# Mask products behind waits on relus and sums, query copies on ScalarE, ranking scratch in another block

## The chip, the cores and the metric

The kernel runs on one core of a Trainium2 chip. A core has five engines with a queue each, worked off in order: TensorE (PE in the profile, with PEld for its weight loads), VectorE (DVE), ScalarE (ACT), GpSimd (POOL) and SyncE (SP, which here only issues DMAs). The engines run at the same time and wait for each other through semaphores. The metric is the device time of one execution in microseconds (us).

## The reference

Two layers on x of shape (2, 256, 64, 64), that is two images of 256 channels and N = 4096 positions. Cut to what matters:

```python
# layer 0: sparsemax attention over the positions
e = prelu(batchnorm(conv3x3(x)))            # 64 channels
sim = einsum('bdn,bdm->bnm', e, e)
sim = sim - max(sim, axis=2)
tau = ...                                   # from the sorted row
p = maximum(sim - tau, 0)
x = einsum('bcn,bnm->bcm', x, p) + x
# layer 1: non-local block
g = g_w x + g_b
a, bsc = query and key scalar of each position   # one number each
f = relu(a[:, :, None] + bsc[:, None, :] + wf_b)
y = (f / N) g
z = batchnorm(wz_w y + wz_b) + x
```

## The kernel before

**What it does for the reference.** A position whose row of `sim` has one large entry only, its own, has a row of `p` that is 1 on the diagonal; layer 0 then gives 2x in that column. The kernel surveys all rows, lists the others (up to 384 an image, three blocks of 128, `KB`), and computes only those exactly. A mask per image holds 2 for the positions that are not listed and 1 for those that are. The output of layer 0 is x times the mask plus what the listed rows add. In layer 1 the relu of a sum of two scalars is worked out without the N x N matrix: keys are ranked, sums of g over the ranked keys are made into a table, and each query fetches one row of the table. In image 1 only 16 of 32 blocks of keys (`NR`) are ranked; the other 16 go through a dense product (`pair_f` on ACT, `pair_py` on PE).

**The order of the work.** No order is written out by hand. The kernel makes a few thousand tasks (`plan.task`), each with a cost on one or two engines, a rank, the tasks it comes after and the buffers it takes; `Plan.run` goes through them in the order of a modelled time and emits the instructions. Of the tasks that could start at about the same time the one with the lowest rank is taken. The ranks of the stages are the twenty numbers `DB, CV1, LS, RW0, ...`. So any new rank, cost or dependency can move instructions on every queue. On the chip only the data dependencies and the order within each queue hold; a task's place in the plan's `after` list makes no wait by itself.

**The stages**, image 0 first, image 1 overlapped with it:

- `conv` and `thresholds`, then `survey` (PE products `sv`, DVE running maxima L524 and row maxima L533, ACT row sums L528).
- `listed`: the list of rows. It writes the mask to DRAM and loads it back over all partitions (`keep_out`, `keep_in` L671, L678), and gathers the listed rows of e and x by indirect DMAs on POOL (L710, L714).
- `rows`: PE products `rw` of the listed rows, ACT copies them into `z_0`, `z_1`, `z_2` (L789), DVE takes eight maxima (L792), `threshold(k)` turns them into a bias `nb` by nine small DVE instructions (L796 to L806, among them the 8-wide `tensor_scalar` of L798), and `relu` (L812 on ACT or L814 on DVE) applies it.
- `doubled`: POOL multiplies x by the mask, eight products of 128 x 1024 an image (L764). In the plan they come after the mask and all relus. The instruction itself reads x and the mask only.
- `attend`: PE products `av` of z (L838), and for each of 8 column blocks and 2 channel halves one DVE sum `into` (L845), which adds the product to x and so waits for the mask product of its columns.
- `project`: g, the key and query scalars (`ga`) by PE (L869 for image 0, L895 for image 1) and DVE (L875, L906).
- `Ranked`: `turn` (L1020, L1021) copies the query column of `ga` and its negative; `keys` (L994 to L1008) makes the keys; they go through PE (`pt_k`, L920), ACT (`row_k`, L924), DRAM (`rd_k`) and come back over all partitions as `kb` (L940). `above` counts, for each block of 128 keys, the keys above it, either on ACT (L1032) or on DVE (L1037, a `tensor_scalar` that also sums up); `ties` (L1051, a DVE instruction with two SBUF inputs) counts equal keys; `place` makes ranks; `scatter` (L1072) writes the rows to DRAM in order of rank. Then `load`, `products`, `sums`, `raised`, `stored` make the table, `segments`, `places`, `counts` find each query's row, `fetch` (L1158) gathers it on POOL, and `taken` and `finish` make the output (L1171 to L963).

**Buffers.** The large tiles share seven blocks, S0 to S6, and a new tile in a block waits for the last use of the one before. Before the change S6 holds the mask of image 0 and then `ga_0`; S3 holds the fourth conv input of both images, later the table of image 1; S5 holds `e_1` (read until the last `rw` of image 1), then the scratch `junk_0` of the ranking of image 0 and then `rest`, the dense part of image 1. The products `rw` of the listed rows use S0, S1, S2 and S4 for z.

Of the kernel before, what the change touches and what calls it, by code (L numbers as in the profile page):

```python
# [8 lines left out]
F32 = mybir.dt.float32  # L9
BF16 = mybir.dt.bfloat16  # L10
# [4 lines left out]
ALU = mybir.AluOpType  # L15
# [4 lines left out]
P = 128  # L20
HW = 64
N = HW * HW
CB = 512
NCB = N // CB
NT = N // P
CT = 2
# [164 lines left out]
def sparse_path(ctx: ExitStack, tc, a, out, rows_i):  # L191
# [89 lines left out]
    DB, CV1, LS, RW0, SV1, RW1, A0, G0, A1, R0, K0, CH0, R1, K1, CH1, P1, P2, SP1, PY, PF = 13.5, 11.59, -11.38, -21.22, -11.5, -7.77, 14.5, -12.16, -19.33, 14.33, -0.92, -6.33, -24.95, -6.8, -0.35, -15.83, -22.49, -13.59, 6.76, -7.17  # L281
    plan = Plan()
    ring_sim, ring_av, ring_y, ring_b = Ring(3), Ring(2), Ring(2), Ring(2)

# [135 lines left out]
    def thresholds(b, e_of, there, rank):  # L420


        et = dram.tile([N, CR], F32, name=f"et_{b}")
        ev = et.rearrange("(j d p) c -> j p d c", d=4, p=P)
        d = {}
        both = {"thr": None, "nthr": None, "lim": None}

        def turned(jp):
            e = e_of()
            ps = d[jp, "ps"] = ps_sim.tile([P, 2, 4, P], F32, name=f"tr_{b}_{jp}", tag="sim")  # L430
            for i in range(4):
                for h in range(2):
                    nc.tensor.transpose(ps[:, h, i, 0:CR], e[ts(h, CR), jp, ts(i, P)], ident[ts(h, CR), ts(h, CR)])

        def copied(jp):
            es = d[jp, "es"] = work.tile([P, 2, 4, CR], F32, name=f"es_{b}_{jp}", tag="wa")
            nc.scalar.copy(es, d[jp, "ps"][:, :, :, 0:CR])  # L437

        def stored(jp):
            for h in range(2):  # L440
                nc.sync.dma_start(out=ev[2 * jp + h], in_=d[jp, "es"][:, h])

        def squared(jp):
            es = d[jp, "es"]
            d[jp, "sq"] = work.tile([P, 2, 4, CR], F32, name=f"sq_{b}_{jp}", tag="wb")
            nc.gpsimd.tensor_mul(d[jp, "sq"], es, es)  # L446

        def limits(jp):
            if jp == 0:
                for n in ("d", "thr", "nthr", "lim"):  # L450
                    both[n] = small.tile([P, NT], F32, name=f"{n}_{b}", tag=n, bufs=2)
            c = both["d"][:, ts(jp, 8)]
            nc.vector.tensor_reduce(c, d[jp, "sq"], AX.X, ALU.add)
            thr = both["thr"][:, ts(jp, 8)]
            nc.vector.tensor_scalar(thr, c, 1.0 - SLACK_REL, -1.0 - SLACK, ALU.mult, ALU.add)
            nc.vector.tensor_scalar_mul(both["nthr"][:, ts(jp, 8)], thr, -1.0)
            lim = both["lim"][:, ts(jp, 8)]
            nc.vector.tensor_scalar(lim, c, 1.5 * SLACK_REL, 1.0 + 1.5 * SLACK, ALU.mult, ALU.add)

        limited, saved = [], []  # L460
        for jp in range(NCB // 2):
            hs, hy, hb = ring_sim.hold(), ring_y.hold(), ring_b.hold()
            t = plan.task({"P": 0.5}, lambda jp=jp: turned(jp), rank, [there[jp]], take=hs)
            t = plan.task({"A": 0.6}, lambda jp=jp: copied(jp), rank, [t], take=hy, free=[hs])
            v = plan.task({"G": 1.1}, lambda jp=jp: squared(jp), rank, [t], take=hb)
            u = plan.task({"D": 1.2}, lambda jp=jp: limits(jp), rank, [v], free=[hb])
            limited.append(u)
            saved.append(plan.task({"S": 0.2}, lambda jp=jp: stored(jp), rank, [t, v], lat=2.6, free=[hy]))
        return et, both, limited, saved
# [154 lines left out]
    def listed(b, et, flag_of, saved, flagged, got, rank, free_mask, free_ec):  # L624
# [47 lines left out]

        def keep_in():
            if b == 0:
                mask = room.tile([P, N], BF16, name=f"mask_{b}", tag="S6")
            else:
                mask = one.tile([P, N], BF16, name=f"mask_{b}", tag="wu")
            nc.sync.dma_start(out=mask, in_=d["kd"].to_broadcast((P, N)))  # L678
            got["mask"] = mask
# [74 lines left out]
        xbs_ready = [T({"A": 0.5}, lambda k=k: x_scaled(k), rank + 5, [fx[k]]) for k in range(KB)]  # L754
        return ecs, xbs_ready, masked, mms

    def doubled(b, got, masked, raw, rank):

        def part(ct, q):
            xq = xs[b][:, ct, ts(q, UN)]
            nc.gpsimd.tensor_tensor(out=xq, in0=xq, in1=got["mask"][:, ts(q, UN)], op=ALU.mult)  # L764

        return {
            (q, ct): plan.task({"G": 2.15}, lambda ct=ct, q=q: part(ct, q), rank, [masked, *raw])
            for q in range(NU)
            for ct in range(CT)
        }  # L770

    def rows(b, e_of, got, ecs, rank, free_z):


# [56 lines left out]
    def attend(b, got, done, halves, xb_ready, rank):  # L831

        pss, last = {}, {}

        def product(j, ct, k):
            if k == 0:
                pss[j, ct] = ps_av.tile([P, CB], F32, name=f"av_{b}_{j}_{ct}", tag="av")
            nc.tensor.matmul(  # L838
                pss[j, ct], lhsT=got["xb"][:, k, ts(ct, P)], rhs=got["zs"][k][:, ts(j, CB)],
                start=(k == 0), stop=(k == KB - 1),  # L840
            )
# [134 lines left out]
    class Ranked:  # L976
# [40 lines left out]

        def turn(self):
            self.a = small.tile([P, 2, NT], F32, name=f"a_{self.b}", tag=f"a{self.b}")
            nc.vector.tensor_copy(self.a[:, 0], self.ga[:, :, CI + 2])  # L1020
# [314 lines left out]
    halves0 = doubled(0, got[0], masked0, list(done0.values()), DB)  # L1335
    flagged1, flag1, sv1 = survey(1, e1_of, both1, there1, copied1, limited1, accs0[1:], SV1, flagged0)
    ecs1, xb1, masked1, ohl1 = listed(1, et1, flag1, saved1, flagged1, got[1], LS, conv1, rw0)
    last0, at0 = attend(0, got[0], done0, halves0, xb0, A0)
    ga0 = []

    def ga0_of():
# [7 lines left out]
    halves1 = doubled(1, got[1], masked1, list(done1.values()), DB + 1)  # L1349
    last1, at1 = attend(1, got[1], done1, halves1, xb1, A1)  # L1350
# [12 lines left out]

    r0 = Ranked(0, None, NT, at(0))
    all0 = list(dict.fromkeys(projected0.values()))
    turn0 = T({"D": 0.3}, r0.turn, R0, all0)
    row0, row0_there = as_row("a0", lambda: ga0[0][:, :, CI + 2], 0, NT, R0 + 1, all0)
    ring_a = Ring(2)
    blocks = {}
# [88 lines left out]
    turn1 = plan.task({"D": 0.3}, r1.turn, R1 + 3, [projected[NT - 1]])  # L1458
    r1.begin(
        R1, [projected[NR - 1]], K1, CH1,  # L1460
        {
# [404 lines left out]
```

## Time and profile before

| | us |
|---|---|
| median of 3 runs | 733.41 (732.14 to 734.09) |
| the profiled execution | 730.27 |
| its span, first to last instruction | 728.5 |

The mean granted clock of TensorE is 0.916 of full speed. Busy time over the span: PE 595.0 us (82%), DVE 557.5 us (77%), ACT 377.1 us (52%), POOL 209.5 us (29%). By stage, in us from the start of the span:

| stretch | work | PE busy | DVE busy | ACT busy | POOL busy | clock |
|---|---|---|---|---|---|---|
| 0 to 191 | loads, conv, survey of image 0 | 172.6 | 147.0 | 87.6 | 47.0 | |
| 191 to 225 | list of image 0, survey of image 1 | 29.17 | 30.95 | 18.17 | 8.01 | 0.88 |
| 225 to 257 | rows of image 0 | 20.57 | 29.75 | 19.74 | 14.63 | 0.84 |
| 257 to 346 | survey of image 1, attend and project of image 0 | 87.92 | 72.16 | 56.19 | 0.00 | 0.98 |
| 346 to 373 | list of image 1, rest of attend and project | 24.85 | 16.22 | 1.34 | 8.16 | 1.00 |
| 373 to 409 | keys of image 0, rows of image 1 | 18.58 | 35.06 | 17.04 | 12.48 | 0.76 |
| 409 to 495 | ranking of image 0, attend of image 1 | 57.12 | 80.25 | 85.36 | 31.86 | 0.87 |
| 495 to 547 | ranking of image 1, dense part | 48.85 | 43.17 | 41.85 | 23.82 | 0.92 |
| 547 to 729 | tables, fetches, outputs, dense part | 135.4 | 103.0 | 49.8 | 63.5 | |

An engine that is busy all through a stretch may still be waiting inside an instruction: a row's time runs from the start of the instruction to its end, and an instruction that is held up after its start shows as a long one. The rows of the timeline, not the sums, tell the two apart.

### The profile page before, as it was taken

The numbers are of one execution on the slowest core, as the hardware profiler recorded it, in microseconds if no ns is written. First come the engines' busy times: TensorE is split into PE (matmuls) and PEld (weight loads), VectorE is DVE, ScalarE is ACT, GpSimd is POOL, SyncE is SP. The second block draws the span as 40 slices with busy tenths as digits, with TensorE's granted clock in tenths as the row PEclk, the third lists the DMA queues.
The fourth block names the chain that finished last, engine by engine and source line by source line (L and its number), as shares of the span: only waits on it lengthen the run. The fifth ranks groups of instructions, "written<-read, shape, count | busy, mean of one in ns | idle before, by whom it ended". The sixth has DMA issues, their size and how long they took to land.

```text
span 728.5 us, 7927 instructions
## 1 busy us (share of the span) xinstructions
PE 595.0 (82%) x2629; PEld 291.7 (40%) x2629; DVE 557.5 (77%) x1060; ACT 377.1 (52%) x525; POOL 209.5 (29%) x256
## 2 busy tenths in 40 slices
PE   5998999999688599999965587936999986494983
PEld 4664444444333233444531232624445452242431
DVE  6976877878998988787769999993997974554154
ACT  0123565675366565675035699996983621330500
POOL 0118920000019100000091043433460047456320
PEclk9999999999899799999996789976998989696998
DMA  9621000101200000000110300006504344483253
GB/s 350 207 58 30 1 15 15 30 1 30 87 3 25 1 0 0 1 1 1 59 28 0 146 18 26 26 19 192 154 28 125 143 171 134 130 280 96 58 172 123
DMA packets 32824, 54.42 MB, mean 75 GB/s; under 512 B 12786, under 2 KB 19812, under 8 KB 31876
## 3 DMA queue, kind: packets, MB, share of 16 engines
q1 hardware_dynamic: 27252, 40.60, 16.5%
q0 software_dynamic: 5088, 12.61, 6.4%
q10 hardware_dynamic: 432, 0.59, 0.3%
q8 instruction: 23, 0.38, 0.2%
q14 instruction: 29, 0.24, 0.1%
HBM read 31.62 MB, written 20.07 MB: 71 GB/s over the span
## 4 chain that ended last, share of the span: by engine, by line
PE 48%; DVE 25%; ACT 13%; issue 5%; DMA 3%; another core or an unknown queue 3%; POOL 0%; SPq 0%; DVEq 0%; ACTq 0%
PE sv L476 15%; ACT junk L1032 11%; PE cv_in L363 6%; PE cv_out L363 6%; PE av L838 6%; PE py L1435 5%; DVE junk L1037 3%; PE pz L956 3%; DVE mq L792 2%; PE g L869 2%; DVE xbs L524 2%; DVE a L1020 2%; DVE tab L1105 2%; DVE x L960 1%
## 5 line engine op out<-in xcount | busy, mean ns | idle before, releaser
L528 ACT ACTIVATE sv<-sv,nthr 128x1024 f32<-128x1024 f32 (+1 forms) x131 | 129.0, 984 | 88.0 <-DVE xbs L524 44.3
L524 DVE TENSOR_TENSOR xbs<-sv,xbs 128x1024 f32<-128x1024 f32 (+1 forms) x120 | 130.7, 1089 | 36.5 <-PE sv L476 27.6
L476 PE MATMUL sv<-e 64*128 64x512 f32 x512 | 135.7, 642 | 3.3 <-ACT sv L528 1.8
L1435 PE MATMUL py<-f,ga 128*128 128x512 f32 x256 | 123.0, 632 | 2.3 <-ACT f L1427 2.3
L838 PE MATMUL av<-z,xbs 128*128 128x512 f32 x192 | 99.4, 653 | 22.6 <-DVE x L845 12.0
L1427 ACT ACTIVATE f<-ab,ga 128x1024 f32<-128x1024 f32 x64 | 72.1, 1144 | 88.5 <-PE py L1435 39.7
L1032 ACT ACTIVATE junk<-kb,bound 128x768 bf16<-128x768 f32 (+30 forms) x51 | 94.8, 1859 | 6.4 <-DMA kb<-rd_k 5.8
L1158 POOL DMA_INDIRECT r<-tb,k x64 | 62.5, 977 | 95.5 <-DVE tab L1105 41.7
L1072 POOL DMA_INDIRECT sg<-ga,rank x48 | 50.3, 1047 | 105.8 <-DVE junk L1051 54.5
L1037 DVE TENSOR_SCALAR_CACHE_REDUCE junk<-kb,ga 128x2048 bf16<-128x2048 f32 (+25 forms) x43 | 77.9, 1847 | 2.5 <-DMA kb<-rd_k 1.9
L1435 PEld LDWEIGHTS py<-f,ga 128*128 128x128 f32 x256 | 50.6, 204 | 59.0 <-issue 55.1
L476 PEld LDWEIGHTS sv<-e 64*128 64x128 f32 x512 | 46.0, 195 | 68.0 <-issue 43.4
L838 PEld LDWEIGHTS av<-z,xbs 128*128 128x128 f32 x192 | 35.9, 203 | 79.7 <-issue 47.4
L960 DVE SCALAR_TENSOR_TENSOR x<-pz,s,x 128x512 f32<-128x512 f32 x32 | 22.8, 747 | 42.3 <-PE pz L956 18.4
L363 PE MATMUL cv_out<-v,wu 128*64 128x256 f32 (+1 forms) x384 | 48.9, 394 | 7.6 <-DVE v L325 7.6
L710 POOL DMA_INDIRECT eb<-et,idx x6 | 6.0, 992 | 149.9 <-issue 124.9
L363 PE MATMUL cv_in<-v,wu 128*64 128x256 f32 (+1 forms) x384 | 46.8, 383 | 1.0 <-ACT c L374 1.0
L446 POOL TENSOR_TENSOR sq<-es 128x512 f32<-128x512 f32 x8 | 8.9, 1108 | 133.8 <-ACT es L437 114.0
L363 PEld LDWEIGHTS cv_out<-v,wu 128*64 128x64 f32 x384 | 28.8, 141 | 30.0 <-issue 12.7
L956 PE MATMUL pz<-yT,wz_sb 128*128 128x512 f32 x64 | 31.4, 630 | 6.5 <-DVE yT L1185 4.9
L363 PEld LDWEIGHTS cv_in<-v,wu 128*64 128x64 f32 x384 | 27.8, 136 | 22.1 <-issue 10.7
L533 DVE MAX8 top<-sv 128x8 f32<-128x1024 f32 x29 | 35.5, 1223 | 0.0
(204 smaller groups left out, 761.8 us busy)
## 6 DMA issues: line engine op xcount, KB each, us to landing
out<-x SPq DMA_DIRECT2D x32, 256.0 KB
tb<-tab SPq DMA_DIRECT2D x3, 2056.0 KB
x<-in_x SPq DMA_DIRECT2D x8, 512.0 KB
tab<-sg SPq DMA_DIRECT2D x3, 1040.0 KB
x<-in_x SPq DMA_DIRECT2D x4, 544.0 KB
e<-e SPq DMA_DIRECT2D x16, 128.0 KB
et<-es SPq DMA_DIRECT2D x16, 128.0 KB
mask<-kd SPq DMA_DIRECT2D x2, 1024.0 KB
```

The lines of the kernel that those rows point to most:

```text
L363: nc.tensor.matmul(d[jp, g][ts(h, CR), n, (r0 - r) * HH : (r1 - r) * HH], lhsT=taps(j, kc, dy), rhs=v[:, kc, r0 + dy - 1 : r1 + dy - 1], s ...
L476: nc.tensor.matmul(ps[:, ts(h, CB)], lhsT=lhs(h), rhs=e[ts(h, CR), q], start=True, stop=True)
L524: nc.vector.tensor_tensor(out=acc[:, cols], in0=d[i, q][:, cols], in1=acc[:, cols], op=ALU.max)
L528: nc.scalar.activation(ps, ps, AF.Relu, bias=both["nthr"][:, i : i + 1], accum_out=got_s["over"][:, i, q : q + 1])
L838: nc.tensor.matmul(pss[j, ct], lhsT=got["xb"][:, k, ts(ct, P)], rhs=got["zs"][k][:, ts(j, CB)], start=(k == 0), stop=(k == KB - 1),)
L956: nc.tensor.matmul(d["z"][:, ct], lhsT=wz_sb[:, ts(ct, P)], rhs=d["y"], start=True, stop=True)
L1032: nc.scalar.activation(self.junk[:, 0, c0:c1], kb[:, c0:c1], AF.Sign, scale=STEEP, bias=self.bound[:, d, t : t + 1], accum_out=cnt[:, t, 3 ...
L1037: nc.vector.tensor_scalar(self.junk[:, 1, c0:c1], kb[:, c0:c1], self.key[:, t : t + 1], None, (ALU.is_ge, ALU.is_gt)[d], ALU.add, accum_ou ...
L1072: rows = nc.gpsimd.indirect_dma_start(out=self.sg, out_offset=bass.IndirectOffsetOnAxis(ap=self.rank[:, t : t + 1], axis=0), in_=self.ga[: ...
L1158: nc.gpsimd.indirect_dma_start(out=self.r[:, t % TH], out_offset=None, in_=self.tb, in_offset=bass.IndirectOffsetOnAxis(ap=self.k[:, t : t ...
L1427: nc.scalar.activation(fm, am, AF.Relu, bias=bm)
L1435: nc.tensor.matmul(pys[q][:, ts(h, CB)], lhsT=ga1[0][:, m, 0:CI], rhs=f[0][:, m % 4, ts(h, CB)], start=(m == NR), stop=(m == NT - 1),)
```

## The change

The parts of the diff, in the order of the code:

```diff
-    DB, CV1, LS, RW0, ... = 13.5, 11.59, -11.38, -21.22, -11.5, -7.77, 14.5, -12.16, -19.33, 14.33, -0.92, -6.33, -24.95, -6.8, -0.35, -15.83, -22.49, -13.59, 6.76, -7.17
+    DB, CV1, LS, RW0, ... = -16.17, 6.58, -12.34, -22.91, -12.37, -25.58, 4.52, -11.7, -8.57, -12.21, -3.49, 3.38, 7.24, 3.51, 6.34, -23.46, 1.78, 11.05, 19.06, -27.14
...
-                mask = room.tile([P, N], BF16, name=f"mask_{b}", tag="S6")
+                mask = room.tile([P, N], BF16, name=f"mask_{b}", tag="S3")
...
-    def doubled(b, got, masked, raw, rank):
-        def part(ct, q):
-            xq = xs[b][:, ct, ts(q, UN)]
-            nc.gpsimd.tensor_tensor(out=xq, in0=xq, in1=got["mask"][:, ts(q, UN)], op=ALU.mult)
-        return {
-            (q, ct): plan.task({"G": 2.15}, lambda ct=ct, q=q: part(ct, q), rank, [masked, *raw])
...
+    def attend(b, got, done, masked, xb_ready, rank, doubling):
+        pss, last, halves = {}, {}, {}
+        def part(q, ct):
+            tick = small.tile([P, 4], F32, name=f"tick_{b}_{q}_{ct}", tag="tick")
+            if q:
+                nc.gpsimd.tensor_copy(tick[:, 0:1], xs[b][:, ct, ds(2 * (q - 1) * CB, 1)])
+            elif ct == 0:
+                for z in got["zs"].values():
+                    nc.gpsimd.tensor_copy(tick, z[:, 0:N:UN])
+            xq = xs[b][:, ct, ts(q, UN)]
+            nc.gpsimd.tensor_tensor(out=xq, in0=xq, in1=got["mask"][:, ts(q, UN)], op=ALU.mult)
...
         for j in range(NCB):
+            if j % 2 == 0:
+                for ct in range(CT):
+                    before = [last[j - 2, ct]] if j else done.values()
+                    halves[j // 2, ct] = plan.task(
+                        {"G": 2.3 if j or ct else 2.8}, lambda q=j // 2, ct=ct: part(q, ct), doubling, [masked, *before]
+                    )
...
         def turn(self):
-            nc.vector.tensor_copy(self.a[:, 0], self.ga[:, :, CI + 2])
-            nc.vector.tensor_scalar_mul(self.a[:, 1], self.a[:, 0], -1.0)
+            nc.scalar.copy(self.a[:, 0], self.ga[:, :, CI + 2])
+            nc.scalar.mul(self.a[:, 1], self.ga[:, :, CI + 2], -1.0)
...
-    ecs0, xb0, masked0, ohl0 = listed(0, et0, flag0, saved0, flagged0, got[0], LS, [weighed], [])
     e1_of, conv1, there1, copied1 = conv(1, parts1, CV1, no_wait)
+    ecs0, xb0, masked0, ohl0 = listed(0, et0, flag0, saved0, flagged0, got[0], LS, conv1, [])
...
-        {"kb": "S0", "tab0": "S0", "tab1": "S6", "r": "S0", "junk": "S5"},
+        {"kb": "S0", "tab0": "S0", "tab1": "S6", "r": "S0", "junk": "S3"},
...
-    r0.begin(R0, [turn0], K0, CH0, {"ab": a_of_0, "rest": None}, rw1)
+    r0.begin(R0, [turn0], K0, CH0, {"ab": a_of_0, "rest": None}, conv1)
...
-        rest_tasks.append(plan.task({"A": 0.95}, lambda q=q: pair_rest(q), PF - 1, [u, *r0.ranked], free=[hq]))
+        rest_tasks.append(plan.task({"A": 0.95}, lambda q=q: pair_rest(q), PF - 1, [u], free=[hq]))
```

- The first mask product of an image now stands behind three small POOL copies ("ticks") that read one element per quarter of each z, and so wait on the chip for all relus. Each product of the next quarter stands behind a tick that reads one column of x written by the first sum of the quarter before.
- The two query copies move from DVE to ACT, for both images.
- The mask of image 0 and then the ranking scratch of image 0 lie in S3. S3 is free when the last conv input of image 1 has been read. `ga_0` has S6 without waiting for the mask products, and `rest` has S5 without waiting for the ranking.
- All twenty ranks are new, so the plan emits many instructions in another order. In POOL's queue the list of image 1 (six gathers) stays behind the eight products of image 0, and the last four products of image 1 now stand between the scatters of image 0. In DVE's queue the eight `ohl` of the list of image 0 (L682) come together instead of between survey instructions, and on PE the products that use them (L694) stand together as well, so `rw` of image 0 stands behind 12 survey units of image 1 instead of 20.

More of the change, by code (lines that the diff above doesn't have):

```diff
@@ L279, in weight_biases @@
         nc.vector.tensor_sub(gb_sb, gb_sb, pc)
-    DB, CV1, LS, RW0, SV1, RW1, A0, G0, A1, R0, K0, CH0, R1, K1, CH1, P1, P2, SP1, PY, PF = 13.5, 11.59, -11.38, -21.22, -11.5, -7.77, 14.5, -12.16, -19.33, 14.33, -0.92, -6.33, -24.95, -6.8, -0.35, -15.83, -22.49, -13.59, 6.76, -7.17
+    DB, CV1, LS, RW0, SV1, RW1, A0, G0, A1, R0, K0, CH0, R1, K1, CH1, P1, P2, SP1, PY, PF = -16.17, 6.58, -12.34, -22.91, -12.37, -25.58, 4.52, -11.7, -8.57, -12.21, -3.49, 3.38, 7.24, 3.51, 6.34, -23.46, 1.78, 11.05, 19.06, -27.14
     plan = Plan()
@@ L755, in listed @@
         return ecs, xbs_ready, masked, mms
-    def doubled(b, got, masked, raw, rank):
-        def part(ct, q):
-            xq = xs[b][:, ct, ts(q, UN)]
-            nc.gpsimd.tensor_tensor(out=xq, in0=xq, in1=got["mask"][:, ts(q, UN)], op=ALU.mult)
-        return {
-            (q, ct): plan.task({"G": 2.15}, lambda ct=ct, q=q: part(ct, q), rank, [masked, *raw])
-            for q in range(NU)
-            for ct in range(CT)
-        }
     def rows(b, e_of, got, ecs, rank, free_z):
@@ L829, in rows @@
         return done, pes
-    def attend(b, got, done, halves, xb_ready, rank):
-        pss, last = {}, {}
+    def attend(b, got, done, masked, xb_ready, rank, doubling):
[9 more added lines that the diff above has]
+            nc.gpsimd.tensor_tensor(out=xq, in0=xq, in1=got["mask"][:, ts(q, UN)], op=ALU.mult)
         def product(j, ct, k):
@@ L1330, in sparse_path @@
     flagged0, flag0, sv0 = survey(0, e0_of, both0, there0, copied0, limited0, accs0, -24, ready)
-    ecs0, xb0, masked0, ohl0 = listed(0, et0, flag0, saved0, flagged0, got[0], LS, [weighed], [])
     e1_of, conv1, there1, copied1 = conv(1, parts1, CV1, no_wait)
+    ecs0, xb0, masked0, ohl0 = listed(0, et0, flag0, saved0, flagged0, got[0], LS, conv1, [])
     et1, both1, limited1, saved1 = thresholds(1, e1_of, there1, -26)
     done0, rw0 = rows(0, e0_of, got[0], ecs0, RW0, lambda k: conv1)
-    halves0 = doubled(0, got[0], masked0, list(done0.values()), DB)
     flagged1, flag1, sv1 = survey(1, e1_of, both1, there1, copied1, limited1, accs0[1:], SV1, flagged0)
     ecs1, xb1, masked1, ohl1 = listed(1, et1, flag1, saved1, flagged1, got[1], LS, conv1, rw0)
-    last0, at0 = attend(0, got[0], done0, halves0, xb0, A0)
+    last0, at0 = attend(0, got[0], done0, masked0, xb0, A0, DB)
     ga0 = []
@@ L1348, in sparse_path @@
     done1, rw1 = rows(1, e1_of, got[1], ecs1, RW1, lambda k: at0 if k else rw0 + sv0)
-    halves1 = doubled(1, got[1], masked1, list(done1.values()), DB + 1)
-    last1, at1 = attend(1, got[1], done1, halves1, xb1, A1)
+    last1, at1 = attend(1, got[1], done1, masked1, xb1, A1, DB + 1)
     attended = list(last1.values()) + at1
     rooms = [
-        {"kb": "S0", "tab0": "S0", "tab1": "S6", "r": "S0", "junk": "S5"},
+        {"kb": "S0", "tab0": "S0", "tab1": "S6", "r": "S0", "junk": "S3"},
         {"kb": "wu", "tab0": "S3", "r": "S3", "junk": "xb"},
@@ L1365, in sparse_path @@
     all0 = list(dict.fromkeys(projected0.values()))
-    turn0 = T({"D": 0.3}, r0.turn, R0, all0)
+    turn0 = T({"A": 0.5}, r0.turn, R0, all0)
     row0, row0_there = as_row("a0", lambda: ga0[0][:, :, CI + 2], 0, NT, R0 + 1, all0)
@@ L1455, in sparse_path @@
             prev.append(u)
-        rest_tasks.append(plan.task({"A": 0.95}, lambda q=q: pair_rest(q), PF - 1, [u, *r0.ranked], free=[hq]))
-    turn1 = plan.task({"D": 0.3}, r1.turn, R1 + 3, [projected[NT - 1]])
+        rest_tasks.append(plan.task({"A": 0.95}, lambda q=q: pair_rest(q), PF - 1, [u], free=[hq]))
+    turn1 = plan.task({"A": 0.5}, r1.turn, R1 + 3, [projected[NT - 1]])
     r1.begin(
```

## The prediction

> **What bounds the kernel now.** I read the chain of waits first. It names the last wait of each stretch, which busy shares cannot.
>
> ```profile
> PE sv L476 15%; ACT junk L1032 11%; PE cv_in L363 6%; PE cv_out L363 6%; PE av L838 6%; PE py L1435 5%; DVE junk L1037 3%; PE pz L956 3%; DVE mq L792 2%; PE g L869 2%; DVE xbs L524 2%; DVE a L1020 2%; DVE tab L1105 2%; DVE x L960 1%
> ```
>
> TensorE holds most of it, the counting of the ranking (ACT L1032) comes next, and a copy of 32 numbers a partition (L1020) holds 2% of 728.5 us, some 12 to 15 us. That copy does nothing that takes so long. The busy time by stretch (start:end, length, then PE, PEld, DVE, ACT, POOL, clock) says where freed time can be used:
>
> ```profile
> 257.00:346.00 89.00, 87.92 (x335) 35.19 (x335) 72.16 (x84) 56.19 (x99) 0.00 (x0) 0.98 0.00 1
> ...
> 373.00:409.00 36.00, 18.58 (x57) 6.84 (x54) 35.06 (x52) 17.04 (x21) 12.48 (x7) 0.76 0.18 71
> ```
>
> PE is full in the first (87.92 of 89), so PE work that starts sooner ends it sooner. In the second PE stands half the time. The timeline (start, length, engine, in brackets the idle time before and its releaser) shows why, first in the rows of image 0:
>
> ```profile
> 222.92 16.72 POOL L764 TENSOR_TENSOR x<-x,mask 128x1024 f32<-128x1024 f32 x8
> ...
> 232.05 7.62 DVE L798 TENSOR_SCALAR z<-m 128x8 f32<-128x8 f32 x1
> ...
> 242.73 2.08 PE L476 MATMUL rw<-e,ec 64*128 64x512 f32 x4 [7.99 <-ACT z L789]
> ...
> 247.43 0.23 DVE L798 TENSOR_SCALAR z<-m 128x8 f32<-128x8 f32 x1
> ```
>
> Eight products of 2.12 us run back to back to 239.64. The 8-wide instruction L798 takes 7.62 us and ends with them, at 239.67; the same line takes 0.23 us at 247.43. DVE is held, z is late, and PE stands 7.99 us. The second place:
>
> ```profile
> 370.80 14.61 POOL L764 TENSOR_TENSOR x<-x,mask 128x1024 f32<-128x1024 f32 x7
> ...
> 372.81 12.64 DVE L1020 COPY a<-ga 128x32 f32<-128x32 f32 x1
> 373.34 4.68 ACT L789 COPY z<-rw 128x1024 f32<-128x1024 f32 x5 [2.90 <-PE rw L476]
> ...
> 386.92 0.40 PE L920 MATMUL pt_k<-ident,ga 128*32 128x128 f32 x1 [10.20 <-DVE ga L1001]
> ...
> 389.38 1.01 ACT L789 COPY z<-rw 128x1024 f32<-128x1024 f32 x1 [11.36 <-PE rw L476]
> ...
> 399.88 0.24 ACT L924 COPY row_k<-pt_k 32x128 f32<-32x128 f32 x1
> ...
> 408.67 3.71 ACT L1032 ACTIVATE junk<-kb,bound 128x4096 bf16<-128x4096 f32 x1 [5.77 <-DMA kb<-rd_k]
> ...
> 507.76 0.19 DVE L1020 COPY a<-ga 128x32 f32<-128x32 f32 x1
> ```
>
> The copy is held over six products, to 385.45; alone, at 507.76, it takes 0.19 us. Behind it stand DVE's key instructions, behind those pt_k on PE, behind that the next rw, and ACT idles 11.36 us for it. The ranking begins at 408.67 at the end of this chain.
>
> **Terms 1 and 2: the two stalls go.** In the changed queues every image 0 product waits for the relus, so L798 can't meet one: 7.62 − 0.23 = 7.4 us. PE's 7.99 us of idle time is the same wait, and the full stretch behind it passes it on. Bounds: 0 (the rows then wait for something else) and −12 (rw stands behind 12 survey units, not 20, and PE idles some 19 us between 191 and 373). I take −7.4, what the row shows. The products then end later, next to the survey of image 1. They cost nothing there as long as DVE has survey work ahead of the first `into` (six L524 of 1.09 and four L533 of 1.22, 11.4 us, against 0.3 of ticks and 4.2 of two products); without that cover it is 4.5 us.
>
> `turn` goes to ACT as two copies of 0.25 us, about the 0.24 of row_k, in ACT's idle time. DVE loses 12.64 − 0.19 = 12.45 us of hold. Since keys, pt_k, rw, z and row_k wait in series on it, `kb` and the first count come about 12.5 us sooner. Followed by hand through the changed queues, with the rows' durations, the gain is 12.5 to 13.7. Lower bound 0, if the keys (L998 in the new numbering) meet a product; but in POOL's queue the products of image 1 stand behind the three ticks that wait for the relus of image 1, and those come after the keys.
>
> **Term 3: the products come back in the ranking.** Image 1's products now run in pairs behind the sums `into`, and the next thing in DVE's queue is `ties` (L1055, was L1051), two SBUF inputs. The trace has one such meeting:
>
> ```profile
> 430.71 2.14 POOL L764 TENSOR_TENSOR x<-x,mask 128x1024 f32<-128x1024 f32 x1
> ...
> 431.69 1.33 DVE L1051 SCALAR_TENSOR_TENSOR junk<-kb,ga,low 128x128 bf16<-128x128 f32 x1
> ...
> 432.95 0.34 DVE L1051 SCALAR_TENSOR_TENSOR junk<-kb,ga,low 128x128 bf16<-128x128 f32 x1
> ...
> 494.75 0.16 DVE L1065 TENSOR_REDUCE rk<-cnt 128x4 f32<-128x8 f32 x1 [3.35 <-ACT junk L1032]
> ```
>
> 1.33 against 0.34: held 1.0 us to the end of one product. Three of the four pairs stand so. A pair is 4.24 us and starts some 0.7 us before the second sum ends. If it breaks after its first product, the hold is about 1.5; if it acts as a block, as the six at 370.80 did, 3.9. I take 2.8. The first pair is waited for by the first `into`: the last relu of z_2 stands behind the first 3.71 us count on ACT, so 3.71 + 1.15 + 0.27 + 2.12 = 7.25 us, against 4.95 of DVE's own counts and 0.6 of relus still to run: 1.7 us idle. Together 1.7 + 3 × 2.8 − 1.0 (already paid) = +9.1; with the ends of the hold 5.2 and 12.4. Against this stand 3.35 us in which DVE now waits for ACT at the ranking's end (last row above) and 1.6 us of image 1's keys that moved behind the last rank. So DVE ends the ranking at −12.5 + 9.1 − 3.35 − 1.6 = −8.4, ACT at −12.5 + 1.15 (the relu) = −11.3, relative to term 1. Products behind scatters cost nothing: between two sums DVE has two counts of 4.3 us, and a burst of four scatters is 5.1.
>
> `above` on DVE (L1041, was L1037) writes an accumulator and never met a product here. Its 3968 elements take 4.34 us, the pace of L792 (1024 in 1.15), and L792 ran unheld at 227.18 beside the products; I take it as not held. The other end: all eight products paid, 8 × 2.12 − 1.0 = 16.0.
>
> The Trainium skill, "SBUF — State Buffer", section "Who interferes with whom", speaks against this part: a DVE instruction with two SBUF inputs contends with a GpSimd one that reads SBUF, and the loser of the shared pair blocks for the whole instruction. By that rule a pair costs at most one product a held instruction, about 1.5, and the sum above would be 5.2; but the 12.64 us row was held over six products, not one, so I stay with the rows.
>
> **Term 4: the rest.** `rest` no longer waits for the ranks, `ga_0` and the scratch change blocks: 0, since the dense part's py (123 us of PE) runs beside them; without that cover rest is 4 × 1.02 us on ACT (L1446). In the tail the last py is now followed by five column blocks of pz instead of nine; from 695 to 720 PE is busy 18.91 of 25 us, so 6.1 us idle: −1 to −3, I take −2.
>
> **Sum.** PE's path through the dense part gains 7.4 + 11.2 = 18.6, DVE's tables in the tail 7.4 + 8.4 = 15.8. The tail ends on the latter: −15.8 − 2 = −17.8. The profiled execution is 730.27; 712.4 after. The median of the runs is 3.1 above that execution, so 715.5.
>
> **What I can't price.**
>
> ```profile
> 626.65 1.41 DVE L960 SCALAR_TENSOR_TENSOR x<-pz,s,x 128x512 f32<-128x512 f32 x2 [15.90 <-remote]
> ...
> 665.45 0.29 DVE L1150 TENSOR_TENSOR above<-pk,a 128x128 bf16<-128x128 f32 x1 [6.67 <-remote]
> ```
>
> Twice in the tail DVE stands, 22.6 us in all, and the trace has no releaser. Both stretches end just after the last of a burst of POOL gathers (622.98 and 662.8), and PE idles 13.92 and 10.68 with them. The bursts stay, so I keep the cost; bounds 0 and double.
>
> **The rivals.** Main case, 0.50: both stalls go and half comes back in the ranking, 715.5 (704 to 724: terms 1 and 3 at their ends).
>
> B, 0.20: the gain is eaten in the ranking. With L1041 held too, 16.0 − 3.35 − 1.6 = 11.1 of the 12.5 is gone; terms 1 and 4 leave 733.4 − 7.4 − 1.4 − 2 = 722.6, and with term 1 at its bound of 0 it is 730. So 723 to 731, always under the median before. For it: DVE is busy 80.25 of 86 us in the ranking. Against: L792 beside products.
>
> C, 0.10: the unexplained stalls shrink, since gathers start at other moments against the output DMAs: 693 to 702. Nothing in the profile favours it beyond their having no visible cause.
>
> D, 0.15, slower: the same stretches grow. Place: DVE behind the gather bursts. Price: up to 22.6 more, 715.5 + 22.6 = 738. It decides once more than 17.9 us is added. For it: both are in the last 120 us, where nothing after them can absorb a delay, and all ranks there are new. Against: the number of gathers is the same.
>
> E, 0.05: the ticks don't hold the products where they should, and L798 and the keys meet them again: 731 to 735, no change. The changed POOL queue speaks against it.
>
> **How the numbers follow.** A measurement of this kernel can tell about 0.3% (2.2 us) from no change. Faster: main, B and C, 0.80; same: E, 0.05; slower: D, 0.15. The range must leave out about 0.2: most of D, half of C. So 697 to 730.
>
> **What would show it.** Right: L783 (was L798) at 0.23 us always; both copies on ACT near 0.25; first ACT count near 388 (408.67 − 7.4 − 12.5); products after relus, then in pairs; L1055 rows of 1.5 to 4.3 us, about three. Wrong: other DVE rows that end with a product, the first table of image 0 less than 10 us earlier, or longer DVE stretches without a releaser in the tail.

## The result and the profile after

| | before | after | ratio, 95% interval |
|---|---|---|---|
| runs of the result, median | 732.14 us | 736.02 us | 1.0063 [1.0043, 1.0083] |
| profiled execution (span) | 730.27 us (728.5) | 735.76 us (734.0) | |
| the same two programs on another chip, median (run g_after below) | 710.48 us | 702.62 us | 0.989 [0.9863, 0.9918] |

The change is 0.6% slower in the result, and 1.1% faster on another chip. The experiments used four chips. On one of them the kernel before reads 730.5 and the changed kernel 735.57, about as in the result. The record doesn't name the chip of the result; "the chip of the result" below means this one (runs a0_again, e6, e7 and e8) and the result itself. On the other three the kernel before reads 710, and no profile taken on those three has the stretches without a releaser in the tail. Ratios are therefore taken within one chip only, and where two chips are set side by side the text says so.

The chain of waits of the changed kernel, by engine and by line:

```profile
PE 54%; DVE 25%; issue 6%; DMA 5%; another core or an unknown queue 4%; ACT 3%; POOL 2%; SPq 0%; DVEq 0%; ACTq 0%; POOLq 0%
PE sv L476 15%; PE av L836 8%; DVE junk L1041 8%; PE py L1437 7%; PE cv_out L363 6%; PE cv_in L363 6%; PE g L873 2%; DVE junk L1055 2%; PE pz L960 2%; DMA kb<-rd_k 2%; PE sv L508 2%; PE pk L1145 2%; DVE mq L777 2%; POOL r L1162 2%
```

The copy that held 2% (`a`) is gone from the list, and in the ranking the chain now runs through the counts on DVE (L1041), not through those on ACT. The dense part (py) has gone from 5% to 7%, and 4% of the span (3% before) ends in something the profile can't name. The same stretches as before, by busy time (PE, PEld, DVE, ACT, POOL, clock):

```profile
257.00:346.00 89.00, 88.69 (x340) 34.39 (x338) 71.65 (x81) 54.59 (x94) 11.13 (x9) 1.00 0.00 1
373.00:409.00 36.00, 24.41 (x88) 10.60 (x87) 31.78 (x63) 26.40 (x33) 5.63 (x9) 0.90 0.21 80
```

In the second one PE works 24.41 us against 18.58 and ACT 26.40 against 17.04: the hold around the keys is gone. The timeline of the changed kernel, at the places shown of before:

```profile
225.51 0.23 DVE L783 TENSOR_SCALAR z<-m 128x8 f32<-128x8 f32 x1
...
242.86 3.75 PE L836 MATMUL av<-z,xbs 128*128 128x512 f32 x4 [5.37 <-DVE z L799]
...
244.47 4.20 POOL L831 TENSOR_TENSOR x<-x,mask 128x1024 f32<-128x1024 f32 x2
...
377.45 0.25 ACT L1024 COPY a<-ga 128x32 f32<-128x32 f32 x1 [1.49 <-DVE ga L879]
377.45 0.22 DVE L998 TENSOR_TENSOR keys<-ga 128x32 f32<-128x32 f32 x1
...
399.40 3.71 ACT L1036 ACTIVATE junk<-kb,bound 128x4096 bf16<-128x4096 f32 x1 [3.97 <-DMA kb<-rd_k]
```

Both held instructions are short now (0.23 for 7.62; the query copy 0.25 on ACT, and the key instruction behind it 0.22 on DVE). But `keys` starts at 377.45, later than the copy's 372.81 before, and the first count starts at 399.40, not near 388. PE has a wait of 5.37 us for the relus (L799) where it waited 7.99 for the copy of z. The tail:

```profile
610.80 0.75 DVE L964 SCALAR_TENSOR_TENSOR x<-pz,s,x 128x512 f32<-128x512 f32 x1 [11.54 <-remote]
...
678.16 0.75 DVE L964 SCALAR_TENSOR_TENSOR x<-pz,s,x 128x512 f32<-128x512 f32 x1 [14.68 <-remote]
...
679.22 0.48 PE L1182 MATMUL yr<-ident,r 128*128 128x128 f32 x1 [15.35 <-DVE r L1175]
679.49 3.62 PE L1437 MATMUL py<-f,ga 128*128 128x512 f32 x4
...
687.12 1.88 PE L1437 MATMUL py<-f,ga 128*128 128x512 f32 x4
...
696.81 15.62 PE L1437 MATMUL py<-f,ga 128*128 128x512 f32 x36
```

Again two stretches without a releaser, 11.54 and 14.68 us (15.90 and 6.67 before). In the second, PE stands 15.35 us although 36 products of the dense part, which need nothing from this wait, are still to come from 696.81: they stand behind `yr` in PE's queue. Afterwards PE runs at half clock for some us (four py in 3.62 us, later four in 1.88).

What each landmark gained or lost (ends in us from the start of the span; the last column compares the changed kernel on a chip without the stretches, run g_after, with e1_turn, which has the order of before, on another such chip):

| | before | after | forecast | measured | without the stretches |
|---|---|---|---|---|---|
| list of image 0 | 215 | 205 | 0 | −10.4 | −10.9 |
| rows of image 0 (last nb) | 256 | 242 | −7.4 | −13.9 | −14.3 |
| last projection of image 0 (ga) | 373 | 377 | −7.4 | +4.6 | +3.2 |
| first count on ACT (start) | 408.7 | 399.4 | −19.9 | −9.3 | −10.9 |
| last rank of image 0 | 495 | 488 | −15.8 | −6.7 | −8.3 |
| last rank of image 1 | 539 | 540 | −15.8 | +0.5 | +0.1 |
| last table stored | 636 | 636 | −15.8 | +0.2 | −4.1 |
| last py | 695 | 712 | −18.6 | +17.3 | +2.5 |
| end of the span | 728.5 | 734.0 | −17.8 | +5.5 | −9.6 |

About 9 us of the row of py is no loss: PE works 18.6 us after the last py before and 9.7 after the change, so 8.9 us of pz and yr now stand ahead of it. The row of the end has this in it.

### The profile page after: what moved, and what is told of

It reads as the page before. It is cut to its first block, busy times and chain, and to the rows that moved or that the text cites. A ratio compares the mean times of both kernels' runs of the same rounds, so it can differ in the third digit from the quotient of the medians.

```text
span 734.0 us, 7973 instructions
## 1 busy us (share of the span) xinstructions
PE 610.9 (83%) x2629; PEld 295.4 (40%) x2629; DVE 538.9 (73%) x1052; ACT 380.4 (52%) x534; POOL 209.0 (28%) x274
## 4 chain that ended last, share of the span: by engine, by line
PE 54%; DVE 25%; issue 6%; DMA 5%; another core or an unknown queue 4%; ACT 3%; POOL 2%; SPq 0%; DVEq 0%; ACTq 0%; POOLq 0%
PE sv L476 15%; PE av L836 8%; DVE junk L1041 8%; PE py L1437 7%; PE cv_out L363 6%; PE cv_in L363 6%; PE g L873 2%; DVE junk L1055 2%; PE pz L960 2%; DMA kb<-rd_k 2%; PE sv L508 2%; PE pk L1145 2%; DVE mq L777 2%; POOL r L1162 2%
## 5 line engine op out<-in xcount | busy, mean ns | idle before, releaser
L528 ACT ACTIVATE sv<-sv,nthr 128x1024 f32<-128x1024 f32 (+1 forms) x133 | 131.2, 986 | 96.7 <-PE sv L508 48.9
L836 PE MATMUL av<-z,xbs 128*128 128x512 f32 x192 | 106.9, 693 | 30.2 <-DVE x L843 16.1
L1437 PE MATMUL py<-f,ga 128*128 128x512 f32 x256 | 127.5, 649 | 0.0
L1036 ACT ACTIVATE junk<-kb,bound 128x1536 bf16<-128x1536 f32 (+26 forms) x52 | 96.8, 1861 | 5.8 <-DMA kb<-rd_k 5.2
L1041 DVE TENSOR_SCALAR_CACHE_REDUCE junk<-kb,ga 128x1664 bf16<-128x1664 f32 (+20 forms) x42 | 75.5, 1834 | 2.6 <-DMA kb<-rd_k 2.1
L836 PEld LDWEIGHTS av<-z,xbs 128*128 128x128 f32 x192 | 38.1, 215 | 94.3 <-issue 61.7
L1076 POOL DMA_INDIRECT sg<-ga,rank x48 | 47.2, 984 | 70.1 <-DVE rank L1070 52.1
L964 DVE SCALAR_TENSOR_TENSOR x<-pz,s,x 128x512 f32<-128x512 f32 x32 | 23.0, 746 | 60.1 <-PE pz L960 28.6
L1182 PE MATMUL yr<-ident,r 128*128 128x128 f32 x64 | 14.0, 307 | 29.9 <-DVE r L1175 16.1
L960 PE MATMUL pz<-yT,wz_sb 128*128 128x512 f32 x64 | 33.5, 664 | 4.7 <-DVE yT L1189 2.1
L831 POOL TENSOR_TENSOR x<-x,mask 128x1024 f32<-128x1024 f32 x16 | 34.4, 2153 | 0.0
```

Source lines behind the costliest of these rows:

```text
L528: nc.scalar.activation(ps, ps, AF.Relu, bias=both["nthr"][:, i : i + 1], accum_out=got_s["over"][:, i, q : q + 1])
L836: nc.tensor.matmul(pss[j, ct], lhsT=got["xb"][:, k, ts(ct, P)], rhs=got["zs"][k][:, ts(j, CB)], start=(k == 0), stop=(k == KB - 1),)
L960: nc.tensor.matmul(d["z"][:, ct], lhsT=wz_sb[:, ts(ct, P)], rhs=d["y"], start=True, stop=True)
L1036: nc.scalar.activation(self.junk[:, 0, c0:c1], kb[:, c0:c1], AF.Sign, scale=STEEP, bias=self.bound[:, d, t : t + 1], accum_out=cnt[:, t, 3 ...
L1041: nc.vector.tensor_scalar(self.junk[:, 1, c0:c1], kb[:, c0:c1], self.key[:, t : t + 1], None, (ALU.is_ge, ALU.is_gt)[d], ALU.add, accum_ou ...
L1076: rows = nc.gpsimd.indirect_dma_start(out=self.sg, out_offset=bass.IndirectOffsetOnAxis(ap=self.rank[:, t : t + 1], axis=0), in_=self.ga[: ...
```

## The experiments

**The copies alone.** The kernel before with one edit (all queues else the same):

```diff
-            nc.vector.tensor_copy(self.a[:, 0], self.ga[:, :, CI + 2])
-            nc.vector.tensor_scalar_mul(self.a[:, 1], self.a[:, 0], -1.0)
+            nc.scalar.copy(self.a[:, 0], self.ga[:, :, CI + 2])
+            nc.scalar.mul(self.a[:, 1], self.ga[:, :, CI + 2], -1.0)
```

> The kernel before with the two query copies issued by ACT and nothing else; the order of all other instructions is that of before. Theory A (the copy is what the products hold, and it alone): L1020 takes 0.25 us on ACT, the keys on DVE start near 373 instead of 385.6, and the time falls by 8 to 12 us. Theory B (the products hold any DVE instruction with two SBUF inputs): the first key instruction L994 is held in the place of L1020 until the seven products end near 385.4, and the time is within 2 us of before.

Measured: 711.26 us against 710.0, 1.0015 [0.9998, 1.0032]. Its timeline:

```profile
372.44 14.61 POOL L764 TENSOR_TENSOR x<-x,mask 128x1024 f32<-128x1024 f32 x7
...
374.35 0.25 ACT L1020 COPY a<-ga 128x32 f32<-128x32 f32 x1 [2.33 <-DVE ga L875]
374.35 12.78 DVE L994 TENSOR_TENSOR keys<-ga 128x32 f32<-128x32 f32 x1
```

ACT copies in 0.25 us and the next DVE instruction takes over the hold, 12.78 us, to the same end of the same products. Moving the victim is worth nothing. L994 has two SBUF inputs. The Trainium skill, "SBUF — State Buffer", section "Who interferes with whom", says that such an instruction contends with a GpSimd one that reads SBUF and that the loser blocks for the whole instruction; the 12.78 us agree with the contention, but they span six products, not one.

**The ticks alone**, for image 0 (e2_tick0), image 1 (e6_tick1) and both (e3_tick01), in the order of before:

```diff
+            if q == 0 and ct == 0 and b in (0,):
+                tick = small.tile([P, 4], F32, name=f"tick_{b}", tag="tick")
+                for z in got["zs"].values():
+                    nc.gpsimd.tensor_copy(tick, z[:, 0:N:UN])
```

> The kernel before with three small POOL copies ahead of the eight products of image 0, which read the z tiles and so wait for their relus; order otherwise as before. Theory A (the stall of L798 is on the path, as the prediction had it): L798 takes 0.23 us in all three blocks, the third z is there 7 to 8 us sooner, the keys of image 0 start 6 to 8 us sooner, and the time falls by 5 to 8 us. Theory B (PE's wait is replaced by the next one): L798 is short all the same, but the keys start less than 3 us sooner and the time is within 2 us of before.

> The kernel before with the three POOL copies ahead of the products of image 1 only; order otherwise as before. If e3's 14.6 us is the stall of L1020 alone, this one gives 11 to 14 us of it (ratio 0.980 to 0.985): L1020 takes 0.2 us and the first ACT count comes 12 us sooner. If the two ticks only work together, it gives less than 8 us.

> As e2, with the same three copies ahead of the products of image 1 too, so that these wait for the relus of image 1. Theory A (both stalls are on the path): L1020 takes 0.2 us, the first ACT count comes 17 to 20 us before that of the kernel before, seven products in a row then hold the first ties L1051 for up to 14 us, and the time falls by 8 to 14 us. Theory B (what is gained before the ranking is given back behind it): the first count comes at least 10 us sooner, but the ranks of image 0 end less than 6 us sooner and the time is between 6 us faster and 4 us slower than before.

Measured: 0.9981 [0.9959, 1.0004], 0.9839 [0.9821, 0.9858] and 0.9793 [0.9763, 0.9824]. Rows of e3:

```profile
233.03 0.23 DVE L802 TENSOR_SCALAR z<-m 128x8 f32<-128x8 f32 x1
...
251.94 16.73 POOL L768 TENSOR_TENSOR x<-x,mask 128x1024 f32<-128x1024 f32 x8
...
268.70 0.57 DVE L879 TENSOR_TENSOR ga<-g,gb_sb 128x393 f32<-128x393 f32 x1 [6.53 <-POOL x L768]
...
372.93 0.21 DVE L998 TENSOR_TENSOR keys<-ga 128x32 f32<-128x32 f32 x1
```

The stall of L798 is gone in e2 and e3 (0.23 us), and the rows of image 0 end 7.9 us earlier in e2 than in e1_turn, but the last projection and `keys` only 3: eight products now run from 251.94 as one block, and the first projection waits 6.53 us for them. Nearly all of what the ticks bring is the second place: the products of image 1 no longer lie under the keys.

**Ticks for both images and the copies** (e8_tick01_turn), on the chip of the result:

> As e3 (relu ticks of both images in the order of before), with the two query copies on ACT. Behind the ticks the copies are 0.37 us of DVE, so this is within 1 us of e3: ratio 0.978 to 0.981.

Measured: 717.65 us, 0.9829 [0.9813, 0.9844]; the changed kernel beside it:

> The changed kernel itself, beside the kernel before on the same chip. Theory S (the stretches without a releaser in the tail, 22.6 us before and 26.2 us after, belong to some executions and not to the kernels, as their absence in the profile of e1 suggests): the tail has no such stretch in either, and since they are about the same in both the ratio stays between 0.998 and 1.008. Theory R (they come with the order of the tail): the changed kernel keeps at least 10 us of them, and its time is over 1.5% above before.

735.57 us, 1.0066 [1.0048, 1.0084]. So the ticks on the relus and the copies, in the order of before, are 17.9 us better than the whole change. **The changed kernel without the ticks on x** (one product after the other in any case, queues the same):

```diff
-            if q:
-                nc.gpsimd.tensor_copy(tick[:, 0:1], xs[b][:, ct, ds(2 * (q - 1) * CB, 1)])
-            elif ct == 0:
+            if q == 0 and ct == 0:
```

> The changed kernel without the ticks on x, so that only the first product of an image waits for the relus and the others follow it as POOL's queue has them; the order is that of the changed kernel. If the pairing of products with sums is what costs (attend of image 1 ends at 468 as in before, though its rows were 7.5 us sooner), the last sum of image 1 comes 4 to 8 us sooner and the time is 4 to 10 us below the changed kernel. If the order of the queues is what costs, the last sum of image 1 and the time stay within 3 us of the changed kernel.

738.16 us, 1.011 [1.009, 1.013]: these ticks aren't the loss. **The changed kernel with the old ranks:**

```diff
-    DB, CV1, LS, ... = -16.17, 6.58, -12.34, ...
+    DB, CV1, LS, ... = 13.5, 11.59, -11.38, ...
```

> The changed kernel with the twenty ranks of the kernel before, so all of the change but the numbers. If the waits and copies are what made the kernel slower, this stays at 735 us or above; if the new ranks (the new order of the queues) did, it is at 731 us or below, and faster than before by what the two stalls are worth (up to 15 us).

782.95 us, 1.1026 [1.0995, 1.1058]. Here `row_k` of image 0 ends 33 us later than in e1_turn, and the ranking with it. The old ranks don't suit the new tasks; the run says that the ranks had to be new, not what the new ones cost.

**The order alone.** e8's program, with its tasks emitted in a recorded order in place of the plan's choice:

```diff
-            at, e, t = min(c, key=lambda x: x[:2])
+            _, e, t, at = min(c, key=lambda x: x[0])
```

where the key is now a task's place in the record. h1_all takes the order of the changed kernel (without the ticks on x); h2_late that of before up to the query copies of image 0 and the changed one after; h3_early the mirror image; h4_tail that of before up to the last rank of image 1.

> The program of e8 (relu ticks, copies on ACT, but the blocks S5 and S6 and the data dependencies of before) with its 1788 tasks emitted in the order of the changed kernel. On each engine the queues are then those of e7. If the order of the queues alone makes the changed kernel slower, this one is as slow as e7 and the changed kernel: ratio to before 1.004 to 1.014. If the blocks or the freed waits cost the time, it stays near e8: 0.980 to 0.988.

> The program of e8, emitted in the order of before up to the query copies of image 0 and in the order of the changed kernel behind them. If the loss is made before the keys of image 0 (5 us later in the changed kernel than in e8), this stays near e8, 0.980 to 0.988; if most of it is made behind (12 of 17 us by the profiles), the ratio is 0.993 to 1.005.

> The mirror of h2: the order of the changed kernel up to the query copies of image 0, that of before behind them. By the profiles the keys of image 0 come 5 us later than in e8 and nothing else is lost: ratio 0.986 to 0.993. If the early order also sets what comes behind, over 1.000.

> The program of e8 in the order of before up to the last rank of image 1 (about 540 us), and in that of the changed kernel behind it. By the profiles the changed kernel loses 5 us between the stored table of image 1 and the end: ratio 0.987 to 0.994. If the tail's order costs nothing by itself, 0.981 to 0.985; if it is better, as the prediction had it, below 0.981.

Measured: 0.9935 [0.9913, 0.9958], 0.9916 [0.9883, 0.9948], 0.9855 [0.9798, 0.9911], 0.9828 [0.98, 0.9857], on a chip without the stretches. e8 itself wasn't run on that chip; on two other such chips e3 (without the copies) has 0.9793 and e8 0.9811 (g_e8 below). Against these the new order costs 1.2 to 1.4% (9 to 10 us) in all. The part from the ranking on costs more (1.1 to 1.2%) than the early part (0.4 to 0.6%, not clear of its interval), and the tail alone (0.2 to 0.4%) lies in the range expected for a tail whose order costs nothing. h1 and h2 fall between their two theories: the order does cost time, but less than the 17.9 us above.

**All on one chip without the stretches:**

> The changed kernel itself, beside e8's program in two orders, all on one chip. Theory A (the order of the queues is about a third of the loss and the releaser-less stretches of its tail are the rest): about 1.0065 where the kernel before reads near 730 with stretches; near 0.993 where it reads near 710 without stretches, like h1. Theory B (the stretches are a mere property of the chip and cost both kernels the same): the same distance to e8 in either case, 17 to 18 us.

> The ticks for the relus of both images and the two copies on ScalarE, everything else in the order before. Both theories: 0.979 to 0.984 on any chip, rows L783/L798 of about 0.23 us, keys unheld. If it reads over 0.99, the gain of the ticks itself depends on the chip.

> e8's program emitted in the changed kernel's order (its scratch blocks are those of the kernel before). If it equals g_after within 0.3%, the scratch blocks cost nothing and the whole loss against g_e8 is the order. If g_after is slower by 0.5% or more, the scratch blocks or the waits they bring cost time. Theory A: g_h1 minus g_e8 is about 10 us without stretches in the tail, 17 with them.

> e8 with eight short memsets on GpSimd ahead of each gather of the fetch, so the gathers of the tail come further apart (1.25 us between them now, over 1.7 then). If the dense burst of gathers makes the stretches without a releaser, those are gone or under 5 us in all, and the time is below g_e8 where g_e8 has them. If they have another cause, they stay at about 20 us in all, and the time is g_e8's plus the later landing of the last rows, 0 to 15 us. Where g_e8 has no stretches, this run says nothing on them, only what pacing costs.

Measured: 702.62 us, 0.989 [0.9863, 0.9918]; 696.62, 0.9811 [0.9781, 0.9842]; 705.04, 0.9928 [0.9907, 0.995]. The scratch blocks and the ticks on x cost nothing that shows: the changed kernel isn't slower than h1's order in e8's blocks. The order costs 6.0 to 8.4 us against e8. On the chip of the result the same distance was 17.9 us, so some 10 to 12 us of the loss there are not the order by itself. e9 put eight memsets ahead of each gather:

```diff
+            pace = small.tile([P, 96], F32, name=f"pace_{self.b}_{t}", tag="pace")
+            for _ in range(8):
+                nc.gpsimd.memset(pace, 0.0)
             nc.gpsimd.indirect_dma_start(
```

807.49 us, 1.138 [1.1341, 1.142], far over the expected 0 to 15 us; its chip showed no stretches to begin with, so it doesn't tell whether the bursts of gathers make them. It is a miss, and the question stays open.

g_after shows what the stretches are worth. It is the very program of the result, and its profile agrees with the one of the result within 0.4 us at every landmark down to 568 us (last rank of image 1 at 540 in both, py of image 0 ended at 568 in both). Its tail, at the instructions that stood in the result:

```profile
595.76 0.75 DVE L964 SCALAR_TENSOR_TENSOR x<-pz,s,x 128x512 f32<-128x512 f32 x1 [0.80 <-PE pz L960]
...
647.17 0.75 DVE L964 SCALAR_TENSOR_TENSOR x<-pz,s,x 128x512 f32<-128x512 f32 x1 [1.57 <-PE pz L960]
```

11.54 us have become 0.80 and 14.68 have become 1.57, and the span is 700.9 us against 734.0. One program, one order, 33.1 us between two chips, all of them after 568 us. The two rows hold 23.9 us of that; the rest lies around them, a part of it in PE at half pace already before the first (four py at 587.29 in 3.76 us, in g_after at 584.69 in 1.96). a0_again, the same program on the chip of the result, has these py in 1.96 us and its stretches elsewhere: DVE waits 4.94 us without a releaser up to 599.61, 13.99 up to 620.09 and 11.30 up to 673.70 (the last two put down to `yr` on PE and to "issue"). Its span is 733.1 all the same. So the total is steady, and the rows in which it shows are not.

For the order of before the like pair is the profile of before (728.5) and e1_turn (710.5), which agree within 3.5 us down to 600 us: 18.0 us. By these spans the stretches cost 15.1 us more in the changed order than in the old one, and −9.6 + 15.1 = +5.5 is the result. That pair is two programs. By the medians of the same program on two chips (a0_again and g_after, with the kernel before of each) it is 33.0 us against 20.0, so 13.0 more, and −7.9 + 13.0 = +5.1.

## Why the prediction was wrong

The forecast of 715.5 us and its sign were wrong for the chip of the result, though rival D named what turned it.

- **"the two stalls go", the first.** L783 takes 0.23 us, as said. The step that failed is the sentence after it: that "the full stretch behind it passes it on". −7.4 us was taken and +4.6 measured at the last projection of image 0 (+3.2 without the stretches), outside the bounds of 0 and −12 on the side of a loss. PE's wait was replaced, not removed: from 191 us to the last projection PE idles 18.1 us against 19.5, now 6.4 of it for relus (3.3 before) and 4.5 for `ohl` (2.2 before). And PE is busy for 168.3 us with the same matmuls that took 162.3, which makes −1.4 + 6.0 = +4.6. The clearest place lies just ahead of the last projection (first before, then after, each with the stretch from 363 to 371 us):

```profile
363.57 5.31 PE L838 MATMUL av<-z,xbs 128*128 128x512 f32 x12
363.00:371.00 8.00, 7.56 (x33) 4.24 (x32) 2.07 (x3) 1.34 (x3) 6.16 (x8) 1.00 0.18 45
...
364.19 0.27 PE L694 MATMUL pj<-val,ohl 128*128 128x9 bf16 x4 [0.34 <-DVE ohl L682]
364.79 0.27 PE L694 MATMUL pj<-val,ohl 128*128 128x9 bf16 x4 [0.33 <-DVE ohl L682]
364.92 8.42 PE L836 MATMUL av<-z,xbs 128*128 128x512 f32 x12
363.00:371.00 8.00, 6.98 (x23) 3.13 (x24) 2.81 (x7) 0.00 (x0) 3.84 (x4) 0.57 0.07 12
```

  Twelve `av` take 8.42 us where they took 5.31, at a granted clock of 0.57 against 1.00, behind short `pj` that each wait for an `ohl`. From 361 to 373 us the clock is 0.72 to 0.86 in all seven profiles with the changed early order and 1.00 in all ten with the old one. That the pauses between the `pj` bring it down is argued from this, not tried. The later products, put at nothing, do cost nothing at the first projection in the changed order: it starts at 260.91 without a wait (269.04 before). In the old order they do: in e2 the rows come 7.9 us earlier and the last projection 2.9, and in e3 the first projection waits 6.53 us for the products that had to move.
- **"the two stalls go", the second.** From `ga` to the end of `keys` the change gains 12.7 us (−8.1 against +4.6); the term said 12.45. The size was right, the agent was not: e1 gives the copies alone 1.0015, e3 the ticks alone 0.9793. What was freed here was freed by the products that left, as the term's own lower bound ("if the keys meet a product") had seen.
- **"the products come back in the ranking".** Held rows of the changed kernel:

```profile
403.30 4.21 DVE L1041 TENSOR_SCALAR_CACHE_REDUCE junk<-kb,ga 128x3840 bf16<-128x3840 f32 x1
404.50 4.22 POOL L831 TENSOR_TENSOR x<-x,mask 128x1024 f32<-128x1024 f32 x2
...
409.42 1.66 DVE L1055 SCALAR_TENSOR_TENSOR junk<-kb,ga,low 128x128 bf16<-128x128 f32 x1
...
424.60 1.91 DVE L1055 SCALAR_TENSOR_TENSOR junk<-kb,ga,low 128x128 bf16<-128x128 f32 x1
...
427.11 1.69 DVE L1070 SCALAR_TENSOR_TENSOR rank<-rk 128x4 uint32<-128x4 f32 x1
```

  The lower three are each held to the end of one product (0.34 and 0.16 us alone): the pair breaks. With two more such rows, 1.01 and 2.21, the holds come to 8.48 − 4 × 0.34 − 0.16 = 6.96 us; with 0.57 of waiting for the first product and without the 1.0 already paid before that is 6.5. 9.1 was taken, with 5.2 and 12.4 as ends. L1041 (accumulating) was not held: 3840 elements in 4.21 us at 403.30, beside products from 404.50 to 408.72, is the pace of 3968 in 4.34. So rival B's own mechanism is refuted. What failed is where the slack was booked: the 3.35 and 1.6 us lie at the end of the ranking of image 0 and were set against the holds. But the held rows stand in DVE's queue between the sums of image 1, and image 1's projection, keys and ranks follow these sums. Its first sum comes 7.7 us earlier than before and its last ends 0.2 earlier: the holds are nearly all of what is lost between (DVE is busy there for 57.75 us against 50.87). Its last rank ends 0.5 us later, where −15.8 was forecast.
- **Term 4.** The tail after the last py is 11.8 us shorter, 8.9 of it moved work and 2.9 of it idle time; −2 was taken. The changed blocks show no cost, as said (g_after against g_h1).
- **"What I can't price".** The cost was kept, "bounds 0 and double". Set against chips without the stretches it is 18.0 us of span before and 33.1 after, close to double; the two rows of DVE by themselves are 22.6 us before and 26.2 after. The result lies 4.3 us behind g_after where the first stretch begins, 16.0 behind it ahead of the second (L1189 at 660.11 against 644.14), 31.0 behind the second (L964 at 678.16 against 647.17) and 33.1 at the end. In the second, PE has nothing in front of `yr`. That is rival D, "the same stretches grow", with its place, and 15.1 us of its 22.6 (13 by the medians). It decided with less than the 17.9 us it was said to need, because the other terms had brought only −9.6. Without the stretches the forecast's direction holds (0.989) at about half its size.

Rival C (the stretches shrink) and E (the ticks don't hold) are refuted by the rows above. One sum of the prediction needs a correction: with the ends it gives for terms 1 and 3 (0 and −12 for −7.4, 5.2 and 12.4 for 9.1), the main case runs from 707.0 to 726.2, not from 704 to 724.

What stays open: what the stretches wait for. They are in every profile from the chip of the result and in none from the others; in them little but GpSimd gathers and DMA goes on:

```profile
668.00:673.00 5.00, 0.00 (x0) 0.00 (x0) 0.00 (x0) 0.44 (x1) 3.78 (x5) 0.50 0.40 105
```

(changed kernel, five us of the second stretch: PE, PEld and DVE at zero, ACT 0.44 us, POOL 3.78 us of gathers, DMA share 0.40). That a place for the stretch with free py in front would have cost less is argued, not tried.

## What to carry to other kernels

Removing a stall on the path is worth only what the next wait leaves. Follow the work that you push back to its own reader before you book the gain: in the old order the first projection then waited 6.53 us for the products. And look at what the engine does with the freed time: here PE idled almost as long for other waits and ran the same matmuls at a lower clock. When one engine's work holds another's instruction, move the work that holds and not the instruction that is held: the copies on ACT gave 0, the ticks 2%. A wait whose cause the profile doesn't name belongs in the sum with its bounds and a look at what stands behind it in each queue, and the version to keep is the small one: the ticks and copies in the old order (e8) beat both kernels on both kinds of chip, 0.9829 [0.9813, 0.9844] and 0.9811 [0.9781, 0.9842].

## What the hardware showed unexpectedly

- One program in one order took 702.62 us on one chip and 735.57 on another. In the profiles the whole difference lies after 568 us, 23.9 of 33.1 us in two rows.
- A hold by GpSimd lasts over a chain of products without a gap: six products, 12.64 and 12.78 us, in the old order; one product, 1.01 to 2.21 us, when the products come in pairs behind ticks.
- After an idle time of 15.35 us PE runs at half pace, with a granted clock of 0.50: four py in 3.62 us, and 1.88 some 8 us later. It also does so without a long idle time: behind short `pj` with pauses of at most 1.07 us the clock falls to 0.57, and twelve av take 8.42 us for 5.31.
